# Two-layer graph attention: seven half products a pair in the projection, and another order at the turn of a tile in layer 1

## The chip, the cores and the metric

The kernel runs on one core of a Trainium2 chip. The metric is device time in microseconds (us), from one launch to its end, given as the median over runs. The engines work side by side, each through its own queue in the order of the program: TensorE (PE in the profile, its weight loads PEld), VectorE (DVE), ScalarE (ACT), GpSimd (POOL) and SyncE (SP). Transfers are issued from the queues of SP, ACT and POOL. A gather, with row numbers that are computed in the kernel, is issued from POOL.

## The reference

A graph of 10,000 nodes with 768 features, 160,000 edges and a self loop for each node goes through two layers of graph attention. The edges are sorted by target. In short:

```python
def gat_conv(x, edges, W, a_src, a_dst, bias, heads, out_ch, concat):
    xl = (x @ W).reshape(n, heads, out_ch)
    alpha_src = einsum('nhc,hc->nh', xl, a_src)
    alpha_dst = einsum('nhc,hc->nh', xl, a_dst)
    e = leaky_relu(alpha_src[src] + alpha_dst[dst], 0.2)
    e = exp(e - segment_max(e, dst)[dst])
    alpha = e / (segment_sum(e, dst)[dst] + 1e-16)
    out = segment_sum(xl[src] * alpha[:, :, None], dst)
    return (concat or mean over heads)(out) + bias

h  = relu(layer_norm(gat_conv(x, W1: 768 -> 4 heads x 256))) + x @ Wr1 + br1
h2 = layer_norm(gat_conv(h, W2: 1024 -> 768, one head)) + h @ Wr2 + br2
out = layer_norm(x + h2)
```

All numbers are float32.

## The kernel before

The nodes are cut into 79 tiles of 128. There are three stages: the projection, layer 1 and layer 2. The change touches the first two; layer 2 runs the same instructions before and after.

**Projection** (the loop over t at L669). For each tile, `product` multiplies the tile's x, which `load_x` has brought in already transposed as six blocks of 128x128, with W1 (six blocks of 128x1024). That makes twelve PE products of 128x128 by 128x512, into two PSUM banks. ACT copies the result to a row in SBUF (L674). DVE multiplies the result, from PSUM, with the two attention vectors (L677), ACT sums each head's 256 columns (L680), and POOL adds the bias (L682). SP stores the row to table1 (L684). Once per tile, `next(steps)` emits one step of two other pieces of work, which so share the engines with the projection: `prepare` builds the list of neighbours of every node, and `weight_steps` loads W2 and Wr1 and forms the attention columns of W2 (L659, L660). Steps of `prepare` that matter here: three counts a step, each of which compares 1408 sorted values per partition with a limit and sums the outcome (L240, DVE), whose results become the row numbers of a gather in the same step (L242, L245); one step with a comparison of 128x5056 and the start of running sums (L272, L277), continued in the next; steps of ranks (L324 to L331); scatters from POOL, six a step (L314); and twenty steps of neighbour lists, four gathers each (`listed`, L366 to L386, with the gathers at L393).

**Layer 1** (`ordered_layer1`). The nodes have been sorted by their number of neighbours, so that the 128 nodes of a tile have about as many: the number of slots of a tile goes from 8 up to 41 in the middle of the run and down to 9. Tiles of 14 to 19 slots are 43 of the 79. The rows of the neighbours (4 KB each) are gathered slot by slot into a ring of 29 (`Ring`, L425). A slot's place is free again once its row has been weighed. For one tile:

- `logits` (L478 to L490) needs all slots of the tile in the ring. It makes the exponents of the attention weights; POOL also takes the rank of each neighbour out of the rows (L489) and writes -BIG over the two attention entries and the rank (L490). `normalised` (L497 to L503) divides by the sum.
- The first `on_pe(t)` slots, one to four, are summed on PE with diagonal matrices of the weights (L739 on ACT, L745 on PE). Of the others, three of four are multiplied by their weights on ACT (L509) and added on DVE (L516), and one of four is done on DVE alone, head by head (L520).
- The last slot is added with an accumulated row sum (L826), from which ACT makes the mean and, with a pass of squares, the deviation (`deviation_about`, L590 to L594). DVE scales, shifts and adds the residual (L603, L605, L854).
- PE transposes h (L717), multiplies x with Wr1 for the residual (L172) and h with W2 in two parts: the first 512 columns in mid tile (`first_columns`, L775) and the last 258 columns at the next turn of a tile (`last_columns`, L790), between the transposes of x and those of the next h. ACT copies both parts out (L783, L796).

The order is written by hand (`manual_schedule`), and every engine follows it. The logits of tile t+1 begin five slots before the end of tile t where the ring has room (`EARLY`, `begin`), and then the first slot of tile t+1 that is not on PE is weighed ahead of the norm of tile t (`begun`). `ps_half` has two PSUM banks, which the transposes and both parts of the product with W2 share.

## Time and profile before

| What | Value |
|---|---|
| Median of 3 runs | 5480.69 us (5478.41 to 5491.34) |
| Profiled execution, its own time | 5480.69 us |
| Its span, first to last instruction | 5478.9 us |
| Mean granted clock of TensorE | 0.939 |
| Projection, products of x with W1 | 9 to 878 us |
| Layer 1 | about 895 to 3580 us |
| Layer 2 | about 3580 us to the end |
| Busy, share of the span | PE 87%, DVE 76%, POOL 60%, ACT 54% |

In the lines of the profile L172 is the line of the kernel, `out<-in` are the names of tiles, xN is a count, and the busy time and the mean duration of one instruction (in ns) follow. What stands behind a bar or in square brackets is the time for which the engine had nothing to do before the instruction, and what ended that time. A float32 product counts as two PE instructions in the profile. A busy share is a mean over stages: which engine a stage waits for has to be read inside the stage.

### The profile page before, as it was taken

The page shows a single profiled execution, that of the slowest core. Times are in us where ns is not written, and L with a number is a line of the kernel's source. Part 1 is how long each engine was busy: PE and PEld are TensorE (multiplying, and loading weights), DVE is VectorE, ACT ScalarE, POOL GpSimd, SP SyncE. Part 2 cuts the span into 40 slices and gives each one's busy share as a digit, 9 for nine tenths or more (in the row PEclk, how much of TensorE's full clock was granted, in tenths as well). Part 3 has the DMA queues.
Part 4 walks back from the last instruction along what each step waited for, and adds up shares of the span by engine and source line. Part 5 has one row for each costly group of instructions (what it writes and reads, how often), then busy time and mean ns, then how long its engine had stood idle before and what let it go on. Part 6 is the DMA issues. An engine that isn't in the chain of part 4 may idle for free. (4 is left out here: it accounts for less than half of the span.)

```text
span 5478.9 us, 58838 instructions
## 1 busy us (share of the span) xinstructions
PE 4753.3 (87%) x14847; PEld 2820.8 (51%) x14847; DVE 4186.5 (76%) x7350; ACT 2936.0 (54%) x8442; POOL 3267.3 (60%) x3407
## 2 busy tenths in 40 slices
PE   8999996998998876578898989999998865889998
PEld 3444443555555543344555545556666544566665
DVE  5784244788888777677788888759988766789998
ACT  3434344777788776677887777623333222233333
POOL 2446465555566655655666555257777666677774
PEclk9999998999999998889999999999999887899999
DMA  4333626899999988688999989589999988999995
GB/s 154 123 99 89 91 92 231 297 322 324 333 352 361 333 312 294 236 303 321 340 368 343 324 316 317 192 325 377 382 366 354 327 301 294 332 347 369 368 383 224
DMA packets 474304, 1591.33 MB, mean 290 GB/s; under 512 B 118327, under 2 KB 122487, under 8 KB 473958
## 3 DMA queue, kind: packets, MB, share of 16 engines
q0 software_dynamic: 322384, 1286.62, 65.7%
q1 hardware_dynamic: 149520, 297.43, 15.9%
q10 hardware_dynamic: 2054, 3.42, 0.2%
q8 instruction: 125, 2.05, 0.1%
q14 instruction: 221, 1.81, 0.1%
HBM read 1431.80 MB, written 177.29 MB: 294 GB/s over the span
## 5 line engine op out<-in xcount | busy, mean ns | idle before, releaser
L425 POOL DMA_INDIRECT ring<-table,slots x2675 | 2630.2, 983 | 1538.8 <-DVE acc L516 362.2
L520 DVE SCALAR_TENSOR_TENSOR acc<-ring,e,acc 128x512 f32<-128x512 f32 (+1 forms) x2506 | 1567.4, 625 | 161.6 <-PE acc L745 85.8
L509 ACT ACTIVATE ring<-ring,e 128x256 f32<-128x256 f32 x3480 | 1421.3, 502 | 0.0
L516 DVE TENSOR_TENSOR acc<-acc,ring 128x1024 f32<-128x1024 f32 x772 | 950.3, 1231 | 209.0 <-ACT ring L509 167.3
L991 PE MATMUL big<-ring,diagonals 128*128 128x256 f32 x2754 | 679.2, 409 | 202.5 <-ACT diagonals L990 183.8
L172 PE MATMUL big<-w,xT 128*128 128x512 f32 x1896 | 825.0, 597 | 26.7 <-DMA w<-in_W_dram 9.9
L172 PE MATMUL big<-wr,xT 128*128 128x512 f32 x1896 | 829.0, 594 | 0.2 <-ACT xT L718 0.2
L1005 PE MATMUL big<-wr,w 128*128 128x512 f32 (+1 forms) x2464 | 823.1, 487 | 0.0
L991 PEld LDWEIGHTS big<-ring,diagonals 128*128 128x128 f32 x2754 | 559.2, 206 | 319.9 <-ACT diagonals L990 223.0
L1005 PEld LDWEIGHTS big<-wr,w 128*128 128x128 f32 x2464 | 470.0, 191 | 329.5 <-issue 297.8
L172 PEld LDWEIGHTS big<-w,xT 128*128 128x128 f32 x1896 | 362.3, 192 | 485.3 <-issue 466.8
L745 PE MATMUL acc<-ring,diagonals 128*128 128x256 f32 x1568 | 399.9, 414 | 230.5 <-ACT diagonals L739 230.3
L172 PEld LDWEIGHTS big<-wr,xT 128*128 128x128 f32 x1896 | 355.3, 191 | 417.5 <-issue 416.8
L775 PE MATMUL half<-w,hT 128*128 128x512 f32 x1264 | 557.7, 594 | 0.0
L745 PEld LDWEIGHTS acc<-ring,diagonals 128*128 128x128 f32 x1568 | 322.7, 209 | 334.2 <-ACT diagonals L739 272.1
L990 ACT ACTIVATE diagonals<-ident,e 128x128 f32<-128x128 f32 x1377 | 410.9, 387 | 140.5 <-DVE e L500 124.7
L790 PE MATMUL half<-w,hT 128*128 128x258 f32 x1264 | 353.7, 441 | 150.4 <-ACT xT L718 150.4
L775 PEld LDWEIGHTS half<-w,hT 128*128 128x128 f32 x1264 | 239.8, 190 | 304.1 <-issue 287.3
L582 ACT ACTIVATE sd<-mv,eps 128x1 f32<-128x1 f32 x159 | 46.6, 293 | 637.3 <-DVE mv L580 637.2
L790 PEld LDWEIGHTS half<-w,hT 128*128 128x128 f32 x1264 | 273.3, 221 | 218.6 <-ACT xT L718 168.8
L677 DVE TENSOR_TENSOR scr<-big,ad_b 128x1024 f32<-128x1024 f32 x79 | 96.8, 1225 | 377.1 <-ACT row L674 377.1
L682 POOL TENSOR_TENSOR row<-row,none 128x1024 f32<-128x1024 f32 x79 | 187.0, 2367 | 265.9 <-ACT row L674 265.5
(184 smaller groups left out, 4062.0 us busy)
## 6 DMA issues: line engine op xcount, KB each, us to landing
ring<-table,slots POOLq DMA_INDIRECT x2675, 6.5
table<-row SPq DMA_DIRECT2D x79, 516.0 KB, 3.7
h_d<-hT SPq DMA_DIRECT2D x79, 512.0 KB, 6.6
w<-h_d SPq DMA_DIRECT2D x77, 512.0 KB, 8.4
table<-row SPq DMA_DIRECT2D x79, 385.0 KB, 6.0
ring<-table SPq DMA_DIRECT2D x79, 385.0 KB, 6.5
xT<-in_x_cols_dram SPq DMA_DIRECT2D x79, 384.0 KB, 4.6
x_d<-xt SPq DMA_DIRECT2D x79, 384.0 KB, 6.6
```

The costliest lines, as they stand in the source:

```text
L172: nc.tensor.matmul(p[:, c:e], aT[:, j, :], w[:, j, c:e], start=(j == 0), stop=(j == k - 1))
L425: nc.gpsimd.indirect_dma_start(out=to, out_offset=None, in_=table, in_offset=bass.IndirectOffsetOnAxis(ap=index, axis=0), **more)
L509: nc.scalar.activation(row[:, s], row[:, s], AF.Copy, scale=e[:, h:h + 1])
L516: nc.vector.tensor_add(acc[:, :c], acc[:, :c], row[:, :c])
L520: nc.vector.scalar_tensor_tensor(acc[:, s], row[:, s], e[:, h:h + 1], (acc if first is None else first)[:, s], op0=OP.mult, op1=OP.add)
L682: nc.gpsimd.tensor_add(row[:, :C1], row[:, :C1], b1_b)
L745: nc.tensor.matmul(acc[:, c:d], diagonals[:, k * H1 + i, :], ring.slot(q + k)[:, c:d], start=(k == 0 and c % BANK == 0), stop=(k == m - 1 ...
L775: nc.tensor.matmul(q, hT[:, j, :], w2[:, j, :BANK], start=(j == 0), stop=(j == K1 - 1))
L790: nc.tensor.matmul(q, hT[:, j, :], w2[:, j, BANK:R2], start=(j == 0), stop=(j == K1 - 1))
L990: nc.scalar.activation(diagonals[:, k % G, :], ident, AF.Copy, scale=e[:, k, :])
L991: nc.tensor.matmul(to, diagonals[:, k % G, :], ring.slot(FIRST[t] + k)[:, ON_PE2:C2], start=False, stop=(k == n - 1), skip_group_check=True)
L1005: nc.tensor.matmul(r[:, c:d], hT[:, j, :], wr2[:, j, c:d], start=False, stop=(j == K1 - 1 and d < C2), skip_group_check=True)
```

## The change

**Projection.** Tile 0 is multiplied as before. After it, tiles go in pairs. The pair's x (two tiles by two halves of the 768 rows) and W1 (two halves of rows by two halves of columns) are taken as 2x2 blocks, and their product is formed from seven block products instead of eight (Strassen's scheme), each of three PE products. DVE forms three sums and two in-place differences of blocks of W1 once, five sums of blocks of x for each pair, and seven combinations of the products into the two rows; ACT copies two of the products. DVE's multiplications with the attention vectors now read the row in SBUF. x is loaded four tiles ahead instead of two, and a pair's loads stand ahead of its stores in SP's queue. Both steps of a pair come at its end. Every second count runs on ACT, as a sum of signs and a small copy that halves it, and a count becomes a row number one step after it was made. Tiles of `prepare` share buffers.

**Layer 1.** The mean and the deviation come from DVE's statistics (`deviation`) again, there is no early first slot, the logits of the next tile begin three slots before the end, and the product with W2 is one piece in mid tile. `on_pe` gives one slot more to PE for tiles of 14 to 19 slots. The last slot is no longer always shared with ACT. What POOL did in `logits` is done by DVE.

```diff
+            def counts(j):
+                for i in range(j, min(j + STEP, NB)):
+                    less = pool2.tile([P, NA * P], BF16, name="less")
+                    if i % 2:
+                        nc.vector.tensor_scalar(less, most..., ids[:, i:i + 1], 0.0,
+                                                op0=OP.is_lt, op1=OP.add, accum_out=whole[:, i:i + 1])
+                        continue
+                    nc.scalar.activation(less, most..., AF.Sign, scale=-1.0,
+                                         bias=halves[:, i:i + 1], accum_out=whole[:, i:i + 1])
+                    nc.scalar.activation(whole[:, i:i + 1], whole[:, i:i + 1], AF.Copy, bias=0.5 * NA * P, scale=0.5)
...
-                nc.gpsimd.tensor_scalar(slots[:, a:b], rows[:, :, R1 - 1], -1.0, float(NP), op0=OP.mult, op1=OP.min)
-                nc.gpsimd.memset(rows[:, :, c + heads:], -BIG)
+                nc.vector.tensor_scalar(slots[:, a:b], rows[:, :, R1 - 1], -1.0, float(NP), op0=OP.mult, op1=OP.min)
+                nc.vector.memset(rows[:, :, c + heads:], -BIG)
...
-        for t in range(NT):
-            p = product(xTs.pop(t), w1, C1)
-            row = io.tile([P, R1], F32, name="row")
-            nc.scalar.copy(row[:, :C1], p[:, :C1])
...
+        def pair(t):
+            a1, a2 = (xTs.pop(i) for i in (t, t + 1))
+            a11, a12, a21, a22 = (a[:, k, :] for a in (a1, a2) for k in (upper, lower))
+            sums = io.tile([P, 5, KH, P], F32, name="sums")
+            for i, (a, op, b) in enumerate(((a11, OP.add, a12), (a21, OP.add, a22), (a11, OP.add, a22),
+                                            (a21, OP.subtract, a11), (a12, OP.subtract, a22))):
+                nc.vector.tensor_tensor(sums[:, i], a, b, op=op)
+            return a11, a22, sums
+        ready = pair(1)
+        for t in range(1, NT, 2):
+            a11, a22, sums = ready
+            r1, r2 = new_row(), new_row()
+            m3 = times(a11, b12)
+            m5 = times(sums[:, 0], b22)
+            nc.scalar.copy(r1[:, right], m5)
+            m2 = times(sums[:, 1], b11)
+            nc.scalar.copy(r2[:, left], m2)
+            nc.vector.tensor_sub(r2[:, right], m3, r2[:, left])
+            m4 = times(a22, b21)
+            nc.vector.tensor_sub(r1[:, left], m4, r1[:, right])
+            nc.vector.tensor_add(r1[:, right], r1[:, right], m3)
+            nc.vector.tensor_add(r2[:, left], r2[:, left], m4)
+            load_x(t + 4)
+            load_x(t + 5)
+            if t + 2 < NT:
+                ready = pair(t + 2)
+            m1 = times(sums[:, 2], bsums[:, 0])
+            nc.vector.tensor_add(r2[:, right], r2[:, right], m1)
+            m6 = times(sums[:, 3], bsums[:, 1])
+            nc.vector.tensor_add(r2[:, right], r2[:, right], m6)
+            times(sums[:, 4], bsums[:, 2], m1)
+            finish(t + 1, r2)
+            nc.vector.tensor_add(r1[:, left], r1[:, left], m1)
+            next(steps, None)
+            finish(t, r1)
             next(steps, None)
...
-                return min(max(SLOTS[t] // 2 - 6, 1), ON_PE1, SLOTS[t])
+                return min(max(SLOTS[t] // 2 - 5, 1), ON_PE1, SLOTS[t])
...
-                return (k - on_pe(t)) % SHARE > 0 or k == SLOTS[t] - 1
+                return (k - on_pe(t)) % SHARE > 0
...
                 if last:
-                    r_before, means, total = last
-                    h = pool.tile([P, C1], F32, name="h")
-                    if total is None:
-                        stats = deviation(small, pieces(means[:, :C1], BANK))
-                    else:
-                        stats, op = deviation_about(small, total, means[:, :C1], h), OP.add
-                begun = first + 1 if whole and early and n - 1 > first else first
-                for k in range(first, begun):
-                    multiplied(k + 1)
-                    weighed(k)
-                    ring.fetch(FIRST[t] + k + 1 + ring.size)
+                    r_before, means = last
+                    stats = deviation(small, pieces(means[:, :C1], BANK))
+                for _ in ahead:
+                    pass
+                if full is not None:
+                    store(t - 2)
                 moves = []
                 if live and t:
                     xT, moves = from_x(t)
-                q = last_columns() if full else None
+                multiplied(first + 2)
+                if last:
+                    h = pool.tile([P, C1], F32, name="h")
+                    scaled(h, [means[:, :C1]], stats, g1_b, be1_b)
+                    nc.vector.scalar_tensor_tensor(h, h, 0.0, r_before[:, :C1], op0=OP.max, op1=OP.add)
                 for move in moves:
                     move()
-                if last:
-                    scaled(h, [means[:, :C1]], stats, g1_b, be1_b, op)
-                    nc.vector.scalar_tensor_tensor(h, h, 0.0, r_before[:, :C1], op0=OP.max, op1=OP.add)
-                multiplied(first + 2)
-                if q is not None:
-                    store(q)
                 multiplied(first + LEAD)
...
                 def to_layer2():
+                    nonlocal full
                     nc.sync.dma_start(h1_d[t - 1], hT.rearrange("p k n -> p (k n)"))
-                    first_columns(t - 1, hT)
+                    full = []
+                    for c in range(0, R2, BANK):
+                        q = ps_half.tile([P, BANK], F32, name="half")[:, :min(BANK, R2 - c)]
+                        for j in range(K1):
+                            nc.tensor.matmul(q, hT[:, j, :], w2[:, j, c:c + q.shape[1]],
+                                             start=(j == 0), stop=(j == K1 - 1))
+                        full.append((c, q))
...
-                    if k >= begin:
-                        ready += list(itertools.islice(ahead, 1))[:2 - len(ready)]
-                    if k >= max(first, begun):
-                        weighed(k)
-                    if k >= begun or k < first:
-                        ring.fetch(FIRST[t] + k + 1 + ring.size)
+                    if n - LEAD <= k < n - LEAD + 2:
+                        ready += itertools.islice(ahead, 1)
+                    if k >= first:
+                        weigh(acc, ring.slot(FIRST[t] + k), e[:, k], DH1, shared=shared(t, k))
+                    ring.fetch(FIRST[t] + k + 1 + ring.size)
```

## The prediction

> **What bounds the kernel now.** I read the page first, then busy time by stage (windows whose edges I took from the first and last start of each line), then the timeline of single tiles. The profiled execution took 5480.69 us, of which its span is 5478.9; it is also the median of the runs (5478.41 to 5491.34), so the sum below goes against 5480.7. The page first: no engine is full over the span, so the stages have to be taken apart.
>
> ```profile
> PE 4753.3 (87%) x14847; PEld 2820.8 (51%) x14847; DVE 4186.5 (76%) x7350; ACT 2936.0 (54%) x8442; POOL 3267.3 (60%) x3407
> L677 DVE TENSOR_TENSOR scr<-big,ad_b 128x1024 f32<-128x1024 f32 x79 | 96.8, 1225 | 377.1 <-ACT row L674 377.1
> L682 POOL TENSOR_TENSOR row<-row,none 128x1024 f32<-128x1024 f32 x79 | 187.0, 2367 | 265.9 <-ACT row L674 265.5
> ```
>
> The windows (us; then busy us and count for PE, PEld, DVE, ACT, POOL; granted clock; DMA share; GB/s). The first four are the projection: PE is near full all along, but DVE's share goes from 22% to 79%. The last two are layer 1, tiles of 15 to 19 and of 20 to 26 neighbours: nothing is full, and DMA is at 0.94 and 0.87.
>
> ```profile
> 24.00:241.00 217.00, 206.10 (x476) 89.89 (x475) 154.66 (x198) 93.66 (x353) 89.39 (x62) 0.98 0.38 120
> 241.00:373.00 132.00, 131.18 (x314) 59.42 (x313) 103.61 (x137) 54.30 (x208) 66.18 (x50) 1.00 0.41 130
> 482.00:640.00 158.00, 158.00 (x369) 69.99 (x369) 35.46 (x31) 66.08 (x263) 87.75 (x70) 1.00 0.49 96
> 640.00:878.00 238.00, 230.94 (x535) 101.86 (x533) 108.02 (x437) 95.08 (x375) 127.16 (x101) 0.99 0.38 88
> 1180.00:1773.00 593.00, 534.28 (x1695) 311.97 (x1693) 505.56 (x770) 471.50 (x1230) 357.83 (x405) 0.96 0.94 340
> 1773.00:2186.00 413.00, 309.10 (x989) 186.77 (x990) 307.22 (x443) 300.23 (x789) 233.16 (x258) 0.90 0.87 316
> ```
>
> DVE's timeline in the first of them. L677 starts 11.45 us apart, not the 10.30 of POOL's L682 in the quiet stage (499.47, 509.77, 520.07): in 16 tiles the counts and the W2 column sums already pace the projection through DVE and ACT.
>
> ```profile
> 199.84 1.23 DVE L677 TENSOR_TENSOR scr<-big,ad_b 128x1024 f32<-128x1024 f32 x1 [1.90 <-ACT row L674]
> 202.11 1.67 DVE L240 TENSOR_SCALAR_CACHE_REDUCE less<-most,ids 128x1408 f32<-128x1408 f32 x1
> ...
> 208.44 0.95 DVE L659 TENSOR_TENSOR scr<-w,a 128x768 f32<-128x768 f32 x1
> 211.29 1.23 DVE L677 TENSOR_TENSOR scr<-big,ad_b 128x1024 f32<-128x1024 f32 x1 [1.90 <-ACT row L674]
> ```
>
> **Part 1, the projection.** PE loses 3 of 24 products a pair. One costs 10.30/12 = 0.858 us, so 2.57 us a pair, 100 us over 39 pairs if nothing else paces. DVE gains 7 operations of 128x512 (L327, the same size: 0.68, spaced 0.61) and 5 of 128x384 (L231: 0.56; plainer, I take 0.48): 6.7 us a pair. ACT's two copies halve (1.05 for 2.0). Half of the counts go to ACT: 80 of 1.72 on DVE become 40, and 40 on ACT that no row shows. From L660 (768 columns 0.84) and L680 (256, 0.40) 1408 columns give 1.4; with read and the halving copy 1.75; bounds 1.5 and 2.0.
>
> The order makes one ring of them, a pair long, because DVE's first subtraction needs ACT's copies of two products, which stand in ACT's queue behind the sums and counts of the last pair: DVE adds m7 (0.61), step one, two multiplications (2.28); ACT sums what the second of these made (1.6 past its half, 3.3 in all), its counts, two copies (1.05); DVE four operations on products (2.44), five sums (2.4), two adds (1.22), two multiplications (2.28). The tail from ACT's copies is 8.35. Before, a pair takes 20.6, and 22.9 where W2's sums run. By stage:
> - start: DVE must change two quarters of W1 after tile 0 read them (1.75 each by L677's rate) before the pair begins: +4, first pair -2;
> - 8 pairs with W2's sums: copies end 16.15 after the m7 add, so 24.5 for 22.9: +13;
> - 6.5 pairs of counts alone: 14.45 + 8.35 = 22.8 for 20.6, +14; the product of br1 with W2 (L172 on brT, 10.3 of PE) now finds PE idle and hides for the most part, -7;
> - 2 pairs with the running sums (64 of 0.19 and one of 5.43, all of them between DVE's parts of the ring): 29 and 27 for 22: +11; 3 pairs of ranks, two chunks of 2.3 us in each step: +5;
> - 5 pairs of scatters: POOL needs 2 x (2.37 + 6 x 1.27) = 20.0: -3; 4 quiet pairs, PE-bound at 18.0: -10;
> - 10 pairs with the lists of neighbours, steps of 2.6 on DVE: here the lock decides.
>
> The lock: L277 takes 0.19 each, but the second of these five started under POOL's add and ended with it:
>
> ```profile
> 383.38 3.13 DVE L277 TENSOR_TENSOR before<-before,hot 128x64 bf16<-128x64 bf16 x5
> 383.41 2.38 POOL L682 TENSOR_TENSOR row<-row,none 128x1024 f32<-128x1024 f32 x1 [7.93 <-ACT row L674]
> ```
>
> So an operation of DVE with two SBUF inputs waits for POOL's 2.37. Now POOL's add starts just ahead of each step, and the list steps are such operations: 2.5 + 2.6 + 2.28, again to 10.0, + 2.6 + 8.35 gives 20.7 for 20.6: +1. Without the lock these pairs run at PE's 18.0: -26. I take the first, as the row shows it.
> The Trainium skill ("SBUF — State Buffer", Who interferes with whom) has the same as a rule: a DVE instruction with two SBUF inputs and a GpSimd instruction that reads SBUF exclude each other for a whole instruction. It speaks against the change more widely than the row does, since the products' rows now lie in SBUF where L677 read PSUM: by the rule each second pair of multiplications also waits up to 1.9 us, in the quiet pairs at no cost (PE still ends last); where DVE paces it would add some 10 us, and the sum of the projection would be +36 for +26.
>
> Sum of the projection: +4 -2 +13 +7 +11 +5 -3 -10 +1 = **+26**, bounds -12 (no lock on the path, -31; counts at 1.5, 0.5 a pair in 14.5 pairs, -7) and +43 (counts at 2.0, +7; ten more from multiplications that wait). Earlier loads and stores hide: x lands in 4.6 us and is wanted a pair later.
>
> **Part 2, layer 1.** Its edits are one design against another. A tile of 17 neighbours:
>
> ```profile
> 1446.45 0.82 PE L717 MATMUL half<-ident,xt 128*128 128x128 f32 x6
> 1450.86 5.43 PE L790 MATMUL half<-w,hT 128*128 128x258 f32 x16 [3.59 <-ACT xT L718]
> 1456.33 0.37 ACT L796 COPY row<-half 128x258 f32<-128x258 f32 x1 [3.65 <-PE half L790]
> 1426.71 1.23 DVE L516 TENSOR_TENSOR acc<-acc,ring 128x1024 f32<-128x1024 f32 x1 [3.15 <-ACT ring L509]
> ```
>
> The last columns of W2's product stand at the turn of the tile: PE waits 3.59 for ACT's copies, ACT 3.65 for that product before it may weight the next rows, and DVE 3.15 for those (the last line is the same place one tile before). After, the whole product runs behind Wr1's, in mid tile, and this chain is gone. What is late next is DVE's own loop. Four neighbours take 2.13 + 3 x 1.33 (L520, L516, by their starts); logits 1.05, weights 1.15; added: slots and -BIG from POOL 0.45 (L489 0.29, L490 0.16), statistics 1.5 (L578, L580: 2 x 0.63 + 0.23) in place of 0.14 on the last add; then scale and residual 3.95. PE's loop: 0.8 + 10.3 + 10.6 + 0.85 + 1.75 a slot + 1.0 wait. One slot more on PE for 14 to 19 neighbours: PE +1.75, DVE -1.4, ACT -0.5. PE's loop is 27.0, 28.8 and 30.5 for two, three and four slots.
> - up to 13 neighbours (14 tiles), PE-bound at 26.0: 25.3 to 26.5, together -3; 14 neighbours (6): 27.0 for 27.2, 0;
> - 15, 16, 17 (23 tiles): 28.6, 28.8, 29.9; now the transposes of h stand 30.4, 30.4, 31.9 apart: -1.8 x 8 - 1.6 x 7 - 2.0 x 8 = -42;
> - 18 and 19 (14): 30.5 and 31.8 for 30.7 and 32.4, with DMA at 0.97 to 0.99: 0.
>
> From 20 on it is another chain, here of 22 neighbours:
>
> ```profile
> 1988.19 0.20 DVE L478 TENSOR_TENSOR e<-ring 128x36 f32<-128x36 f32 x1 [5.46 <-DMA ring<-table,slots]
> ...
> 1996.23 1.23 DVE L826 SCALAR_TENSOR_TENSOR acc<-ring,acc 128x1024 f32<-128x1024 f32 x1
> ...
> 2001.90 2.06 DVE L520 SCALAR_TENSOR_TENSOR acc<-ring,e,acc 128x256 f32<-128x256 f32 x4 [4.37 <-PE acc L745]
> 2003.87 1.28 DVE L603 SCALAR_TENSOR_TENSOR h<-acc,less,g 128x1024 f32<-128x1024 f32 x1
> ```
>
> DVE waits 5.46 for rows that could be asked for only when ring slots came free, and 4.37 for PE before the early first neighbour, with the norm (3.95) queued behind it. After, the norm fills that wait. The loop from PE's sums: 17.0 to free the slot, 8.5 to its landing, logits 1.5, one neighbour 1.33, weights 1.25, then PE's 16 products 10.8 (PE's row here is 9.76, later by the second half of the diagonals, which waits for the deviation): 40.4 for 42.0; 37.8 for 40.2 at 21; 33.2 for 35.3 at 20. The logits come two neighbours later, which the wait for DMA absorbs. 6, 4 and 4 tiles: -12, -10, -6; 23 and 24 (4): -8; the four largest 0.
>
> Sum -81. Loops added from rows leave waits out and the gathers move closer to a full DMA, so I take three quarters, **-60**; bounds -90 and +10.
>
> Together 5480.7 + 26 - 60 = **5446.7, say 5446**.
>
> **The rivals.**
> 1. *Layer 1 does not move* (slower): gathers land as late as DMA lets them. For: 0.94 DMA. Against: tiles of 18 run at 0.98 and 362 to 373 GB/s. Landing of 11 for 8.5 takes the gain of the large tiles, ACT 3 us late at the turn that of the middle ones: 5480.7 + 26 = 5507.
> 2. *PE paces the 43 tiles of 14 to 19* (slower still): each pays the slot, 43 x 1.75 = +75, and gains nothing; -31 stays for the rest: 5550. It decides once PE's wait for ACT's copies at the turn exceeds some 3 us; for it speaks the diagonals' second half, queued behind the deviation.
> 3. *The seven products pay*: DVE keeps up, no lock on the path, counts cheap: half to most of 100 arrives, -60 for +26: 5361. Against: DVE at 79% before 6.7 us a pair are added.
> 4. *The change does nothing in the projection* (0, not +26): 5421.
>
> **How the numbers follow.** Forecast 0.45, rival 1 0.20, rival 2 0.10, rival 3 0.10, rival 4 0.15. What a measurement can tell is 0.3%, 16 us: below 5464 is faster, above 5497 slower. Faster: 0.45 x 0.8 + 0.10 + 0.15 = 0.61; same: 0.45 x 0.15 + 0.04 of rival 1 = 0.11; the rest, 0.28, slower. The range leaves out most of rivals 2 and 3: 5385 to 5530; the forecast's own is 5410 to 5480.
>
> **What would show it.** Projection: L674's successor copies and DVE multiplications 24 to 25 us apart a pair while counts run, 18 in the quiet stage, 20 to 21 with the lists; its end near 905 for 878. Layer 1: no PE wait over 2 us for xT copies; tiles of 15 to 17 at 28.6 to 30 us; no DVE wait for PE's sums ahead of the norm. Wrong if DVE's wait for ACT's weighting stays, if the wait for gathered rows grows past 8 us, or if pairs run at 18 with counts in them.

## The result

The changed kernel takes 5409.5 us (median of four runs, 5396.95 to 5410.77) beside 5481.67 us for the kernel before (four runs): a ratio of 0.986, 95% interval 0.9841 to 0.9879. The gain is 72 us where the forecast had 35. Direction and range held, and by luck: the two terms of the sum did not hold, and their errors of +55 and -88 us cancel in part. The projection costs about three times what was forecast, and layer 1 gains well over twice as much. In some of the runs below layer 2, the same program throughout, takes 2182 to 2198 us instead of 1909 to 1915 and the kernel before 5777 to 5792 us instead of 5482 to 5487, so each run is read by its ratio to the kernel before in the same group, and by stage.

I cut both profiled executions (5480.69 and 5409.06 us) at the same two events, the first transposes of h on PE (tile 0 of layer 1 turns into tile 1) and the last ones.

| Stage | before, us | after, us | difference | forecast |
|---|---|---|---|---|
| to the first transposes of h ("projection" below) | 942.6 | 1023.9 | +81.4 | +26 |
| first to last transposes of h ("layer 1") | 2618.7 | 2470.8 | -147.9 | -60 (raw sum -81) |
| the rest (layer 2) | 1917.7 | 1912.5 | -5.2 | 0 |

On the page of after, DVE is the engine whose busy share rises most (84% for 76%), and its idle time before the adds of rows that ACT has weighted falls from 209.0 to 77.8 us (of which ACT's weighting ended 167.3 before and 8.8 now).

```profile
PE 4704.8 (87%) x14957; PEld 2814.3 (52%) x14957; DVE 4568.7 (84%) x8123; ACT 2826.2 (52%) x8306; POOL 3263.4 (60%) x3159
L528 DVE TENSOR_TENSOR acc<-acc,ring 128x1024 f32<-128x1024 f32 x801 | 985.7, 1231 | 77.8 <-ACT ring L521 8.8
```

The windows of after (us; then busy us and count for PE, PEld, DVE, ACT, POOL; granted clock; DMA share; GB/s). The first three are projection: four pairs with counts and W2's sums, four with counts alone, eight with lists of neighbours. The last two are layer 1, tiles of 15 to 19 and of 20 to 26 neighbours.

```profile
166.10:271.80 105.70, 82.64 (x168) 34.90 (x166) 87.55 (x120) 57.25 (x190) 47.85 (x33) 0.89 0.34 115
308.30:404.90 96.60, 79.67 (x169) 33.99 (x168) 81.13 (x114) 51.64 (x181) 45.16 (x33) 0.93 0.29 93
...
755.50:934.10 178.60, 154.76 (x337) 66.22 (x336) 147.28 (x417) 58.10 (x261) 106.85 (x80) 0.94 0.28 82
...
1254.00:1818.00 564.00, 539.12 (x1831) 323.41 (x1831) 518.73 (x848) 433.68 (x1166) 351.90 (x344) 1.00 0.97 356
1818.00:2200.00 382.00, 303.35 (x988) 183.89 (x986) 327.69 (x502) 283.01 (x753) 227.64 (x226) 0.90 0.93 344
```

In the projection PE, near full before, is idle for a fifth of the time while counts run, and DVE is at 83%: PE has three products fewer a pair, and nothing comes of it. In layer 1 the first window lasts 564 us for 590 before, PE at 96% and granted 1.00, and DMA moves 356 GB/s for 340.

Where the projection's time went is seen in one pair with W2's sums. The last of a pair's seven products is accumulated onto the first one, so PE can begin it only when DVE has read the first (L750), and DVE then adds it (L755). The timeline of after, DVE first, then ACT, then PE (start, us, engine, line, instruction; in brackets the idle time and what ended it):

```profile
140.52 0.69 DVE L755 TENSOR_TENSOR row<-row,m 128x512 f32<-128x512 f32 x1 [2.39 <-PE m L704]
...
150.30 1.73 DVE L253 CAST at<-whole 128x3 int32<-128x3 f32 x1
...
156.18 0.69 DVE L740 TENSOR_TENSOR row<-m,row 128x512 f32<-128x512 f32 x1 [2.24 <-ACT row L739]
...
166.10 0.69 DVE L755 TENSOR_TENSOR row<-row,m 128x512 f32<-128x512 f32 x1 [1.18 <-PE m L704]
...
155.10 0.56 ACT L737 COPY row<-m 128x512 f32<-128x512 f32 x1
155.56 0.58 ACT L739 COPY row<-m 128x512 f32<-128x512 f32 x1
...
150.85 5.31 PE L704 MATMUL m<-bsums,sums 128*128 128x512 f32 x12
161.79 4.27 PE L704 MATMUL m<-bsums,sums 128*128 128x512 f32 x6 [5.63 <-DVE row L750]
```

From one add of the seventh product (L755) to the next are 25.6 us. ACT's copies end 15.6 us after the first of them, where the forecast had 16.15. From there to the next add of the seventh product it had 8.35; the trace has 10.0. Of the difference of 1.6 us, 1.18 is DVE's wait for the seventh product: PE has stood idle for 5.63 us, waiting for DVE's add of the first product, and then three products take 4.27 us where six took 5.31. (At the rate of those six, an estimate, three would have been done 0.5 us before DVE was ready to add them.) The granted clock shows it, over the idle stretch and over the product after it:

```profile
156.20:161.70 5.50, 0.00 (x0) 0.00 (x0) 5.46 (x10) 0.00 (x0) 0.00 (x0) 0.96 0.51 169
161.79:166.10 4.31, 4.31 (x7) 2.02 (x8) 3.05 (x4) 2.28 (x11) 0.95 (x1) 0.66 0.00 0
```

Two more places cost much at once. The pair in which the product of br1 with W2 stands takes 36.5 us, since DVE adds two of its columns in the same step (timeline of after):

```profile
290.29 0.16 DVE L673 TENSOR_TENSOR lift<-row 128x1 f32<-128x1 f32 x1 [12.59 <-ACT row L672]
```

And DVE waits for the gathered windows of the neighbour lists, which one step asks for and the next wants (groups of instructions from 140 us to the end of the projection; busy and mean ns, then the idle time before them and what ended it):

```profile
L385 DVE TENSOR_TENSOR less<-window,named 128x80 f32<-128x80 int32 (+13 forms) x20 | 11.2, 561 | 34.1 <-DMA window<-in_src_dram,begin 34.1
```

In layer 1 the view of waits, tiles of 15 to 19, shows what went. Before (us in total, times, longest):

```profile
PE half L790 <- ACT xT L718: 48.4, 19, 4.5
DVE acc L516 <- ACT ring L509: 51.8, 36, 4.5
ACT row L796 <- PE half L790: 59.7, 20, 5.0
```

and after, where no wait of DVE for ACT's weighting is left among them:

```profile
PE half L790 <- ACT xT L791: 10.1, 17, 1.0
PE acc L818 <- ACT diagonals L812: 8.2, 14, 0.8
...
DVE acc L532 <- PE acc L818: 4.8, 9, 0.6
```

### The profile page after: what moved, and what is told of

Same layout as the page of the kernel before. It is cut to its first block, busy times and chain, and to the rows that moved or that the text cites. A ratio compares the mean times of both kernels' runs of the same rounds, so it can differ in the third digit from the quotient of the medians.

```text
span 5407.2 us, 59694 instructions
## 1 busy us (share of the span) xinstructions
PE 4704.8 (87%) x14957; PEld 2814.3 (52%) x14957; DVE 4568.7 (84%) x8123; ACT 2826.2 (52%) x8306; POOL 3263.4 (60%) x3159
## 5 line engine op out<-in xcount | busy, mean ns | idle before, releaser
L521 ACT ACTIVATE ring<-ring,e 128x256 f32<-128x256 f32 x3284 | 1337.8, 508 | 0.0
L528 DVE TENSOR_TENSOR acc<-acc,ring 128x1024 f32<-128x1024 f32 x801 | 985.7, 1231 | 77.8 <-ACT ring L521 8.8
L911 PE MATMUL half<-w,hT 128*128 128x512 f32 (+1 forms) x2528 | 830.4, 486 | 0.0
L818 PE MATMUL acc<-ring,diagonals 128*128 128x256 f32 x1912 | 477.9, 407 | 194.7 <-ACT diagonals L812 194.4
L818 PEld LDWEIGHTS acc<-ring,diagonals 128*128 128x128 f32 x1912 | 385.5, 205 | 279.9 <-ACT diagonals L812 219.8
L692 ACT ACTIVATE scr<-scr 128x256 f32<-128x256 f32 x632 | 253.5, 403 | 488.9 <-DVE scr L689 488.9
L1022 ACT ACTIVATE diagonals<-ident,e 128x128 f32<-128x128 f32 x1377 | 411.0, 387 | 141.5 <-DVE e L512 128.9
L704 PE MATMUL m<-bsums,sums 128*128 128x512 f32 x702 | 360.6, 665 | 128.5 <-DVE row L750 128.5
L812 ACT ACTIVATE diagonals<-ident,e 128x128 f32<-128x128 f32 x956 | 293.0, 387 | 202.4 <-DVE e L512 202.4
L498 ACT ACTIVATE e<-e 128x68 f32<-128x68 f32 (+29 forms) x160 | 38.2, 239 | 631.5 <-DVE e L497 602.8
L704 PEld LDWEIGHTS m<-bsums,sums 128*128 128x128 f32 x702 | 144.1, 211 | 329.6 <-issue 165.3
```

Source lines behind the costliest of these rows:

```text
L521: nc.scalar.activation(row[:, s], row[:, s], AF.Copy, scale=e[:, h:h + 1])
L528: nc.vector.tensor_add(acc[:, :c], acc[:, :c], row[:, :c])
L704: nc.tensor.matmul(to, a[:, k, :], b[:, k, :], start=(p is None and k == 0), stop=(k == a.shape[1] - 1), skip_group_check=True)
L812: nc.scalar.activation(diagonals[:, k * H1 + i, :], ident, AF.Copy, scale=e[:, k, i:i + 1])
L818: nc.tensor.matmul(acc[:, c:d], diagonals[:, k * H1 + i, :], ring.slot(q + k)[:, c:d], start=(k == 0 and c % BANK == 0), stop=(k == m - 1 ...
L911: nc.tensor.matmul(q, hT[:, j, :], w2[:, j, c:c + q.shape[1]], start=(j == 0), stop=(j == K1 - 1))
```

## The experiments

Fifteen kernels ran, in five groups (runs 1 to 4, 5 to 8, 9 to 12, 13, and 14 with 15), each group beside the kernel before. The projection of after takes 1023.9 to 1029.1 us in the executions that leave it alone, and its layer 1 2467 to 2475.

**1 and 2. Each half alone.** The first kernel keeps the projection of before and takes layer 1 of after; the second does the reverse.

> The projection of before with layer 1 of after. Theory A, read off the two traces: the stages add up, the projection pays 81 us and layer 1 gains 148, the rest 5; then this kernel takes 5481 - 148 - 5 = 5328 us (5315 to 5345). Theory B: the sizes of the forecast (+26 and -60) were right and the stages help each other, layer 1 running better because of what the new projection leaves behind (clock, transfers); then it takes 5400 to 5420.

> The projection of after with layer 1 of before. Theory A: 5481 + 81 = 5562 us (5550 to 5575), slower than before by 1.5%. Theory B, the forecast's +26: 5507 us (5495 to 5515).

Measured: layer 1 alone 0.9714 of before (0.9687 to 0.9741), projection 946.3 and layer 1 2472.3 us; projection alone 1.0143 (1.0117 to 1.0169), projection 1029.1 and layer 1 2636.7. On the time of before the ratios give 5325 and 5560 us, near the 5328 and 5562 of theory A. The stages add up: by the medians of their group (5616.79 and 5864.98 beside 5777.02 us) the differences are -160 and +88 us, together -72, what the change does; by the ratios they are -157 and +78, together -79. The projection of after is a loss, and the sizes of the forecast fall, not its additivity.

**3. Lists two steps behind their gathers.**

```diff
-                for r in asked:
-                    listed(*r)
-                asked = [(t, window)]
+                while len(asked) > 1:
+                    listed(*asked.pop(0))
+                asked.append((t, window))
                 yield
-            yield
```

> After, with each list of neighbours made two steps behind its gathers instead of one. Theory A: DVE waits 34 us in all for the windows (10.9 in the first of the ten pairs, 1.1 to 3.7 in the others), because the two steps of a pair stand 3 us apart; that goes, the pairs come down to 20 to 21 us, and the kernel gains 20 to 34: 5375 to 5389 us. Rival: the lock between DVE's list operations and POOL's add paces these pairs, as the forecast had it; then only the first pair gains, and the time is 5400 to 5409.

Measured: 0.9819 of before (0.9794 to 0.9844), projection 1010.9 us, a gain of 13 and so between the two, nearer to the rival: the first pair with lists comes from 32.9 to 19.0 us, and the next eight only from 22.3 to 21.8 on the mean. No wait for a window is left, but DVE's busy time in those pairs rises from 18.4 to 20.6 us. Beyond the first pair the wait was only taking the place of something else.

**4. ACT's sums behind the next pair's copies.** The sums and the store of the pair's last row are put off until ACT has copied two products of the next pair, and one of the two steps stands ahead of the other row's multiplications. (`finish` is split for this: it keeps the multiplications and POOL's add, and `sums_and_store` has the rest.)

```diff
             nc.scalar.copy(r2[:, left], m2)
+            sums_and_store(*late)
...
-            finish(t + 1, r2)
+            next(steps, None)
+            sums_and_store(*finish(t + 1, r2))
             nc.vector.tensor_add(r1[:, left], r1[:, left], m1)
             next(steps, None)
-            finish(t, r1)
-            next(steps, None)
+            late = finish(t, r1)
```

> After, with ACT's sums of a pair's last row (and its store) put behind the two copies of the next pair, and one of the two steps put ahead of the multiplications of the other row. Theory A, the ring: DVE waits for ACT's copies behind those sums and counts (2.2 to 5.2 us a pair in most pairs); the waits go, pairs with W2's sums come from 26.5 to about 24, pairs with counts alone from 24.1 to 22, scatters from 21.3 to 20; in all -20 to -45, 5365 to 5389 us. Rival: what paces the pairs is DVE's own work with POOL's add in its way (22 us busy, some 2 us more that no wait explains); then the waits only move to another place and the time stays within 8 us of 5409.

Measured: 0.9693 of before (0.9667 to 0.9718), projection 937.3 us. The gain of 87 us there is twice what I expected of the ring. A pair with W2's sums in its timeline, DVE then PE:

```profile
134.71 0.68 DVE L761 TENSOR_TENSOR row<-row,m 128x512 f32<-128x512 f32 x1
...
142.37 0.68 DVE L745 TENSOR_TENSOR row<-m,row 128x512 f32<-128x512 f32 x1
...
156.20 0.68 DVE L761 TENSOR_TENSOR row<-row,m 128x512 f32<-128x512 f32 x1
...
147.96 5.49 PE L708 MATMUL m<-bsums,sums 128*128 128x512 f32 x6 [3.20 <-DVE row L755]
```

Neither the subtraction that wants ACT's copies (L745) nor the add of the seventh product (L761) waits any more: 21.5 us a pair for 26.4, of which DVE is busy 21.1. PE still idles and still runs its next products slowly, but the moved step lies over that. DVE's own work is the bound.

**11. The moved step alone.** Only the first half of that edit: the step moves, ACT's order stays.

> After, with only the first of a pair's two steps moved, from behind the add of the seventh product to ahead of the multiplications of the pair's other row; ACT's order of sums and copies stays. Theory A: the seventh product comes late because PE, after an idle of 5 us, runs it at a lower clock (4.3 us for 2.6); the moved step covers that wait (1.2 to 2.4 us a pair) and no more, since the ring through ACT's copies is as long as before: projection 1024 - 30 = 994 us (985 to 1005). Rival: what the fourth run gained (87 us) came from the moved step and not from ACT's order: projection below 960 us.

Measured: 0.9845 of before (0.9829 to 0.9862), projection 1018.1 us, a gain of 6 where I expected 30. The wait for the seventh product is gone, but the order now puts the first multiplication of one row beside POOL's add for the other, and it takes 3.59 us for 1.22 (DVE and POOL, the same stretch of the timeline):

```profile
149.57 3.59 DVE L689 TENSOR_TENSOR scr<-row,ad_b 128x1024 f32<-128x1024 f32 x1
...
149.71 2.36 POOL L694 TENSOR_TENSOR row<-row,none 128x1024 f32<-128x1024 f32 x1
```

POOL's add starts 0.14 us behind the multiplication, by the profile's start times, and the multiplication ends 1.09 us behind the add. The run changes two things, one of them not meant, and so says little of the ring. Runs 14, 10 and 15 separate them.

**14. ACT's sums put off, the steps left alone**, from the twelfth pair on: the first and last lines of run 4's edit.

> After, with ACT's sums of a pair's last row (and its store) behind the two copies of the next pair, from the twelfth pair on, where W2's sums are done; the steps stay where they are. Theory A, the ring through ACT's queue paces: in the pairs with counts alone the wait for the copies (2.2 us) goes, 24.1 comes down to 22 us, the 1.4 us of the late seventh product stay; scatters and lists gain up to 1 us a pair; projection 1024 - 15 to 35 us. Rival, the late seventh product and POOL's add pace: these pairs stay at 23.5 us and more, projection 1015 or more.

Measured: 0.9803 of before (0.9778 to 0.9828), projection 1004.7 us, 19 less and so inside theory A's range. The pairs with counts alone come from 24.1 to 20.9 us, more than the 2.2 of the wait: the wait for the seventh product, which theory A let stay, went too. ACT's order alone takes the ring away there; DVE, busy for 20.1, is the bound, with no wait from one add of the seventh product (L762) to the next in its timeline. PE, of which the last line is, now idles 2.15 us instead of 5.63 ahead of that product, and its three PE products take 2.84 us instead of 4.27:

```profile
352.41 0.68 DVE L762 TENSOR_TENSOR row<-row,m 128x512 f32<-128x512 f32 x1
...
364.13 0.68 DVE L747 TENSOR_TENSOR row<-m,row 128x512 f32<-128x512 f32 x1
...
372.84 0.68 DVE L762 TENSOR_TENSOR row<-row,m 128x512 f32<-128x512 f32 x1
...
369.72 2.84 PE L708 MATMUL m<-bsums,sums 128*128 128x512 f32 x6 [2.15 <-DVE row L757]
```

**10. No add of the bias.** POOL's add is left out, and with it the addition of b1 to the projected rows.

```diff
-            nc.gpsimd.tensor_add(row[:, :C1], row[:, :C1], b1_b)
```

> After, without POOL's add of the bias b1 to the projected rows (a part of the computation is left out). Theory A, the lock of the forecast: operations of DVE that stand still beside this add (a cast of 3 columns takes 1.7 us beside it and 0.17 elsewhere) are on the ring; without it the pairs with counts lose 1.5 us each and the pairs with lists up to 2.6: projection 1024 - 26 - 20 = 978 us (965 to 1000). Rival, the ring runs through ACT's queue and PE, and what DVE loses beside the add it would spend waiting for ACT's copies: projection 1012 to 1026 us.

Measured: 0.9757 of before (0.974 to 0.9773), projection 963.7 us. Its windows, for the same kinds of pairs as above (with W2's sums, counts alone, scatters, lists):

```profile
165.30:271.00 105.70, 82.62 (x168) 34.91 (x166) 81.67 (x121) 57.24 (x191) 27.81 (x24) 0.89 0.34 115
307.50:404.00 96.50, 79.58 (x169) 33.95 (x168) 74.75 (x113) 51.53 (x181) 24.77 (x24) 0.93 0.28 93
556.40:647.30 90.90, 90.90 (x212) 39.42 (x211) 58.50 (x81) 37.68 (x171) 36.92 (x33) 1.00 0.39 103
734.00:879.80 145.80, 145.80 (x338) 63.20 (x338) 134.14 (x416) 58.07 (x261) 76.05 (x63) 1.00 0.34 100
```

Each theory holds in a stage of its own, and neither total does (965 to 1000 and 1012 to 1026 were expected). In the pairs with counts, where theory A had a gain of 1.5 us each, DVE is busy 6 us less over each stretch, and the stretch is as long as in after to 0.1 us: DVE spends on waits what it saves beside the add. In the pairs with lists and scatters PE is full, 18.2 us a pair, and 18.0 is what the forecast named for a pair without the lock. Not all of the 4.1 us that go from a pair with lists are the lock. DVE's busy time falls by 1.6 us a pair (147.28 and 134.14 over eight pairs); its waits for windows, 19.4 us over the eight pairs in after, are gone as well, and in after POOL's add stands in the same queue that asks for the windows.

**15. The moved step, without POOL's add**: the edits of runs 11 and 10 together, so that b1 is again not added.

> After, with the step moved ahead of the multiplications of the other row (as in the eleventh run) and without POOL's add of the bias (left out of the computation, as in the tenth). Measured against the tenth run, where pairs with W2's sums take 26.3 us, pairs with counts alone 24.1, and the projection ends at 964. Theory A, the late seventh product is a term of the ring: the moved step covers it, pairs come to 24.3 and 22.7 us, projection 964 - 25 = 940. Rival, the ring through ACT is as long without that wait, DVE only waits longer for the copies: 26 and 24 us stay, projection 955 or more.

Measured: 0.9744 of before (0.9722 to 0.9766), projection 938.8 us. Theory A, to 0.2 us: 24.5 and 22.8 us a pair, the two numbers of the forecast's ring, with the wait for the copies still in it (timeline of DVE).

```profile
166.91 0.68 DVE L755 TENSOR_TENSOR row<-row,m 128x512 f32<-128x512 f32 x1
...
177.57 0.69 DVE L739 TENSOR_TENSOR row<-m,row 128x512 f32<-128x512 f32 x1 [3.53 <-ACT row L738]
...
191.42 0.68 DVE L755 TENSOR_TENSOR row<-row,m 128x512 f32<-128x512 f32 x1
```

So the ring without that wait is as long as forecast, and what the forecast lacked was the late seventh product.

The pairs side by side, in us from one add of the seventh product to the next (means over the pairs of a kind, without the first of those with W2's sums, 24.0 in after, and the last with lists; the moved step brings each kind about one pair earlier):

| Pairs | forecast | after | run 3 | run 4 | run 14 | run 11 | run 10 | run 15 |
|---|---|---|---|---|---|---|---|---|
| counts and W2's sums | 24.5 | 26.4 | 26.3 | 21.8 | 26.6 | 26.8 | 26.3 | 24.5 |
| br1's product | 22.8 and a rest | 36.5 | 36.9 | 34.1 | 37.5 | 37.9 | 36.5 | 35.7 |
| counts alone | 22.8 | 24.1 | 24.2 | 20.4 | 20.9 | 25.2 | 24.1 | 22.8 |
| scatters | 20.0 | 21.3 | 21.3 | 20.4 | 20.6 | 20.5 | 18.2 | 18.4 |
| quiet | 18.0 | 18.3 | 18.3 | 18.4 | 17.8 | 18.5 | 18.2 | 18.2 |
| first with lists | 20.7 | 32.9 | 19.0 | 24.5 | 29.3 | 25.7 | 32.1 | 25.6 |
| other lists | 20.7 | 22.3 | 21.8 | 20.3 | 22.3 | 21.1 | 18.2 | 18.5 |

**5. The product with W2 in two pieces at the turn again**, on after's layer 1.

```diff
                 moves = []
                 if live and t:
                     xT, moves = from_x(t)
-                multiplied(first + 2)
+                q = last_columns() if full else None
+                for move in moves:
+                    move()
                 if last:
...
-                for move in moves:
-                    move()
+                multiplied(first + 2)
+                if q is not None:
+                    store(q)
```

> After, with the product with W2 cut in two again: 512 columns in mid tile, 258 at the turn of a tile between the transposes of x and those of h, and the order of the turn that goes with it (copies of x's transposes ahead of the norm and of the first weighted rows). Layer 1 took 2471 us in after and 2619 in before. Theory A, the forecast's reason: this chain at the turn (PE waits for ACT's copies, ACT for that product, DVE for ACT) was what the old order paid for, so layer 1 goes back by 60 to 110 us, tiles of 15 to 17 neighbours to 30 us and more, and PE waits over 2 us for the copies of xT again. Rival, the gain came from the slot moved to PE, or from what moved between POOL, ACT and DVE: less than 30 us are lost here, and more than 60 in one of the next three.

Measured: 1.0177 of before (1.016 to 1.0194); layer 1 takes 2648.9 us, 178 more than after, where 60 to 110 were expected, and 30 more than before. Of the chain that the forecast named, two links are there again, in the waits of the tiles of 15 to 19 neighbours: ACT waits for the last columns, and DVE for ACT's weighting. The third is not: PE waits at most 1.0 us for the copies of xT, where theory A had over 2.

```profile
ACT row L861 <- PE half L855: 37.4, 19, 2.0
ACT xT L791 <- PE half L790: 36.4, 16, 4.3
...
DVE acc L528 <- ACT ring L521: 51.2, 40, 2.7
...
PE half L855 <- ACT xT L791: 10.4, 19, 1.0
```

Tiles of up to 15 neighbours lose next to nothing (0.2 us on the mean), those of 16 and 17 lose 2.2 to 2.6 us each, those of 18 to 20 3.5 to 5, and larger ones 2.6 to 3.7. That is in good part not where the forecast had put the gain: it had 0 for 18 and 19.

**6. One slot fewer on PE**, as before: `SLOTS[t] // 2 - 6` for `- 5`.

> After, with the number of slots summed on PE back to that of before (one fewer for tiles of 14 to 19 neighbours and for those of 20 to 22 as far as the cap allows). Theory A, DVE's own loop paces the tiles of 15 to 19 in after: each pays 1.0 to 1.4 us, layer 1 loses 35 to 60 us. Rival, PE paces them in after: each gains up to 1.75 us, layer 1 gains 20 to 75.

Measured: 0.9955 of before (0.9938 to 0.9972); layer 1 2525.5 us, a loss of 55. Theory A holds for 14 to 19 neighbours (1.2 to 1.4 us a tile from 15 to 17, 0.8 to 0.9 at 18 and 19, 2.0 at 14). From 20 to 22 nothing moves; there the cap of four slots on PE (`ON_PE1`) gives the same number either way. PE now waits for h, which comes from DVE (waits in the tiles of 15 to 19):

```profile
PE half L790 <- DVE h L889: 27.0, 12, 2.4
PE acc L818 <- ACT diagonals L812: 19.1, 14, 2.6
```

**7 and 8. Two moves to DVE undone**: the two small operations of logits on POOL again, and the mean from the last add with ACT's pass of squares again.

> After, with the two small operations of logits (ranks out of the gathered rows, -BIG over their ends) back on POOL. Theory A, DVE's loop paces: DVE is rid of 0.45 us a tile, layer 1 gains 10 to 25 us. Rival, POOL's queue matters: the same queue issues the gathers, the operations wait there for ACT's exponents and hold up the gathers behind them; then layer 1 loses 10 to 60 us, and DVE's or PE's waits for gathered rows grow.

> After, with the mean taken from the sums of the last add on DVE and the deviation from a pass of squares on ACT, and the last slot always shared with ACT, as before. Theory A, DVE's loop paces: DVE is rid of 1.4 us a tile, and ACT, with room, takes 1.3 more: layer 1 gains 20 to 60 us. Rival, what matters is when the deviation is there: ACT's pass stands ahead of the weighting of the next rows and the norm waits for it; layer 1 stays within 10 us or loses up to 60.

Measured: 0.9816 (0.98 to 0.9833) with layer 1 at 2450.8 us, and 0.9837 (0.9821 to 0.9853) with 2459.1 us. Theory A holds for the first, 20 us; the second gives 12, less than its range, and gains it at 15 to 17 neighbours while those of 20 lose 0.7 us a tile. Both moves were small losses inside the change: 1.8% and 1.6% faster than before stand beside the change's 1.4%. The 12 us are not much beside the 8 by which layer 1 of after varies between runs.

**12. The early logits and the early first slot again.**

```diff
+                begun = first + 1 if whole and early and n - 1 > first else first
+                for k in range(first, begun):
+                    multiplied(k + 1)
+                    weigh(acc, ring.slot(FIRST[t] + k), e[:, k], DH1, shared=shared(t, k))
+                    ring.fetch(FIRST[t] + k + 1 + ring.size)
...
-                    if n - LEAD <= k < n - LEAD + 2:
+                    if k >= begin:
```

> After, with the logits of the next tile begun five slots before the end of a tile again, and its first slot that is not on PE weighed ahead of the norm, where the ring has room. Theory A, the forecast's chain for 20 neighbours and more: DVE waits there for PE's sums with the norm queued behind, so each of those 18 tiles loses 1.5 to 3 us, and tiles of 15 to 19 lose 0 to 1: layer 1 2471 + 30 to 60 us. Rival, that wait was only due to the product at the turn: layer 1 stays within 10 us of 2471 or gains.

Measured: 1.0584 of before (1.0566 to 1.0602); layer 1 2862.7 us, a loss of 392 where I expected 30 to 60, and not in the tiles that I had named: those of 11 to 19 neighbours lose 5.4 to 7.4 us each, those of 20 lose 3.6, 21 to 23 1.2 to 2.8, and those of 24 and more nothing. DVE waits for PE's sums of the next tile with the norm behind it, and PE then waits for h (waits in the tiles of 15 to 19):

```profile
PE half L791 <- DVE h L896: 97.6, 18, 5.4
...
DVE acc L533 <- PE acc L819: 133.1, 19, 8.5
```

So the parts of layer 1, undone one at a time, give +178, +392, +55, -20 and -12, which is far from 148.

**13. Both of the turn's parts back together**, the edits of runs 5 and 12.

> After, with both put back: the product with W2 cut in two with its order of the turn (as in the fifth run) and the early logits and first slot (as in the twelfth). Theory A, the two belong together: PE, which in the twelfth run waited 5.4 us a tile for h, has the 5.4 us of the last columns to do there, and what is left is the old order's own chain. Counted back from before by the other parts (2619 - 55 + 20 + 12), layer 1 takes 2596 us (2570 to 2620), less than with either alone. Rival, each costs by itself: layer 1 takes 2863 us or more.

Measured: 1.0062 of before (1.0042 to 1.0081), layer 1 2580.7 us: less than with either alone, and in the range of theory A. PE's wait for h is small again, for the last columns stand in it, and so is DVE's for PE's sums (the same tiles):

```profile
PE half L791 <- DVE h L909: 15.4, 13, 1.2
...
DVE acc L533 <- PE acc L819: 15.8, 15, 1.8
DVE acc L529 <- ACT ring L522: 4.0, 11, 0.6
```

The old order was one design; the change replaced both parts at once, and that was worth 110 us (2580.7 to 2470.8). With 55 for the slot, less 20 and 12 for the two moves, 133 of the 148 us are accounted for; 15 are not. By number of neighbours, in us a tile (from one group of transposes of h to the next):

| Neighbours | tiles | before | after | run 5: W2 split | run 12: early slot | run 13: both | run 6: slot back |
|---|---|---|---|---|---|---|---|
| 9 to 13 | 13 | 26.30 | 24.91 | 25.10 | 30.89 | 26.18 | 24.89 |
| 14 | 6 | 27.40 | 26.16 | 26.46 | 33.60 | 27.49 | 28.16 |
| 15 to 17 | 23 | 30.94 | 28.79 | 30.44 | 34.64 | 28.99 | 30.05 |
| 18 and 19 | 14 | 31.55 | 30.82 | 35.09 | 37.41 | 31.53 | 31.68 |
| 20 to 22 | 14 | 38.62 | 36.03 | 39.50 | 38.65 | 39.25 | 35.92 |
| 23 to 26 | 6 | 45.46 | 42.79 | 46.23 | 43.76 | 46.09 | 43.32 |

**9. What helped, together**: the edits of runs 3, 4 and 7 (not that of run 8), and br1's sum taken by DVE a step later, from two columns that ACT copies for it.

> After, with four edits: the sums behind the copies and the step moved (as in the fourth run), the lists two steps behind their gathers (as in the third), br1's attention sum taken by DVE a step later than ACT copies its product, and the two small operations of logits on POOL (as in the seventh). Theory A, the stages and the edits add up: projection 937 - 6 (the one window wait that is left) - 9 (DVE's wait of 12.6 us for br1's product, less what PE itself needs) = 922 us; layer 1 2451; layer 2 as before: 5288 us (5275 to 5305), a ratio of 0.965. Rival, DVE is the bound of the projection by now and the waits only change places: 937 stays, 5303 us or more.

Measured: 5295.08 us (5292.27 to 5297.55), 0.965 of before (0.9634 to 0.9666), so 2.1% less than the change. Layer 1 2448.1, layer 2 1912.3 us. The projection, 935.3 us instead of 922, is all that fails: the wait for br1's product only changes its place, to the buffer from which that product reads, and the windows' wait had little left to give. The timeline of DVE in that pair:

```profile
252.81 1.23 DVE L691 TENSOR_TENSOR scr<-row,as_b 128x1024 f32<-128x1024 f32 x1 [11.07 <-PE m L670]
```

With these edits the new projection is worth 942.6 - 935.3, 7 us, where PE saves 100, and 7 us is little beside the 4 by which the projection of before differs between its two profiles (942.6, and 946.3 in run 1). DVE paces most pairs.

## Why the prediction was right and wrong

**The projection, +26 for +81.** The mechanism was right: a ring through DVE and ACT while counts run (run 14 opens it), POOL's add in the way of the lists (run 10), PE pacing only the quiet pairs (18.3 measured, 18.0 forecast). The step that failed is the sizing of four terms; the differences are sums over the pairs of each kind.

- "The tail from ACT's copies is 8.35" holds no wait for the seventh product. It measures 10.0 in the pair shown; over eight pairs with W2's sums 209 us for 196, over those with counts alone 5 more. Run 15, with that wait covered and no lock, has the forecast's 24.5 and 22.8. I took PE's products at their full clock in a stage where my own ring, 24.5 us for 18.0 of products, left PE idle for 6 us a pair.
- "Now finds PE idle and hides for the most part, -7": the product does not hide, as DVE takes its result in the same step. One pair of 36.5 for 22.8 and a rest of about 3, 10 to 14 us. I looked for PE's idle time and not for who reads the product.
- "+1" for the lists took the lock alone. The first of those pairs adds 12 us for gathers that the next step wants at once (without that wait, in run 3, the pair takes 19.0 us instead of 32.9), the other nine 1.6 each. The two steps of a pair stand closer together than the steps of two tiles did; the forecast moved the steps and did not follow the gathers that they issue.
- The running sums, ranks and scatters came out at 59.6, 74.5 and 106.7 us for 56, 67 and 100: 18 together.

That makes some 74. Against it stand the first pair and the one behind the counts, 40 us for the 52 that the forecast's stages leave over. So the pairs explain about 62 where the sum was 55 short (911 us from the first add of a seventh product to the last, for some 850), and the rest, in the start and the end, I have not taken apart. The forecast's sign for the end was the last product of x with W1 near 905 us; it ends at 956.

Two sums of the forecast are off by a little: 29 and 27 for 22 twice are +12, not +11, and the lower bound takes 31 for the lock where its own lines give 27.

The forecast also weighed a rule of the Trainium skill ("SBUF — State Buffer", Who interferes with whom): by it, each second pair of multiplications should wait for POOL's add. In after they have a median of 1225 and 1218 ns, so most don't (six of the 138 after 140 us take 3.0 to 4.0 us): in the pair shown, they run while POOL has no add under way (they end at 148.79, and its add starts at 149.63). Run 11, where the two start within 0.14 us of each other, shows the rule: 3.59 us. The rule was right and the order of the two engines in this kernel kept it out. What does stand still in after is an operation that I had not priced, the cast of three counts to row numbers: 1.73 us beside POOL's add as the median of 14, 0.17 in the other 13. The same section of that page names copies and casts among the operations that can take the shared ports; for this cast the trace agrees. In the pairs with counts it costs nothing, by run 10.

**Layer 1, -60 for -148.** Taking "three quarters" of the sum was the first wrong step, and cost 21 us: the forecast's reason was that loops made from rows leave out waits, but the waits of the old order went too. The second is in the raw sum: -81 is little over half of what was measured, since it has nothing for tiles of 14, 18 and 19 neighbours and for the four largest, and too little for those of 9 to 13 and from 20 on. By the tiles:

| Neighbours | forecast, raw | measured | what the runs show |
|---|---|---|---|
| 9 to 13 | -3 | -18 | the turn (run 13: -1.5 with the old one) |
| 14 | 0 | -7 | slot and turn |
| 15 to 17 | -42 | -49 | the slot on PE; the turn adds 5 (run 13: -45) |
| 18 and 19 | 0 | -10 | the turn (run 13: 0) |
| 20 to 22 | -28 | -36 | the turn (run 13: +9) |
| 23 to 26 | -8 | -16 | the turn (run 13: +4) |
| 27 and 41 | 0 | -11 | over half the turn (run 13: -5) |

(Measured is from before to after, in us over all tiles of the row.)

The signs that the forecast named for layer 1 came: in the tiles of 15 to 19 neighbours no wait of PE for the copies of xT is over 1.0 us, and those of 15 to 17 take 28.2 to 29.7 us, for 28.6 to 30. They don't tell the causes apart.

For 15 to 17 neighbours the number was near and the reason wrong. "This chain is gone" was to give the 42; but with the old order of the turn back and all else of the change kept (run 13), these tiles still gain 45, and without the extra slot on PE (run 6) 29 us of the gain go. In run 13 two waits of that chain are small although its order is there: PE waits 3.6 us for the copies of xT and DVE 4.0 for ACT's weighting, where before had 48.4 and 51.8; ACT still waits 36.6 us for the last columns. Beside the slot it keeps the two moves to DVE, the deviation's pass off ACT among them; what of the shrunken waits is due to each was not separated. For 20 neighbours and more the sizes were short by a quarter to a half, and the reason is only in part shown. DVE's wait for PE's sums does fall, as forecast, and its wait for rows too (35.5 to 19.8 us, tiles of 20 to 26). But the early first slot does not bring the first one back: in run 12 it is 11.9 us, and what returns is the wait for rows. The same tiles in before, after and run 12 (the last two lines):

```profile
DVE acc L520 <- PE acc L745: 21.6, 6, 4.5
...
DVE acc L532 <- PE acc L818: 8.9, 9, 1.7
...
DVE e L491 <- DMA ring<-table,slots: 35.6, 10, 5.6
DVE acc L533 <- PE acc L819: 11.9, 8, 2.7
```

And W2's split alone costs these tiles more than the early slot alone: 3.5 us a tile for 2.6 from 20 to 22 neighbours, 3.4 for 1.0 from 23 to 26, where both together cost 3.2 and 3.3. The forecast's chain is thus one of two, and not the larger. That the early slot alone costs 392 us, 349 of them in tiles of up to 19 neighbours, the forecast could not see, since in the old order the product at the turn lay in PE's wait.

"0" at 18 and 19 neighbours, for a DMA share of 0.97 to 0.99, was wrong by 10 us: over the tiles of 15 to 19 DMA still went from 340 to 356 GB/s. The operations from POOL and the statistics were rightly counted as costs of DVE; they are 20 and 12 us (runs 7 and 8).

**The rivals.** 1 (layer 1 does not move) and 4 (the projection costs nothing) fall with runs 1 and 2. 2 (PE paces the tiles of 14 to 19 with its added slot, +75) is refuted by run 6, by which the slot gains 55. 3 (the seven products pay) falls for this order of ACT's queue, and with the order of run 9 the projection as a whole gets 7 us.

## What to carry to other kernels

Work taken off the engine that is full comes to nothing where it is paid in operations of an engine that closes a ring with another one: write down the ring, queue by queue, with the wait at each hand-over, before counting the saving; here the new projection lost 81 us in one order of ACT's queue and its steps and came out even, within 5 to 7 us, in another. A step that is moved takes its gathers along, so look for who wants what it asks for, and when. And parts of a tuned order should not be judged one at a time: two that cost 178 and 392 us alone cost 110 together, because the one filled the wait that the other made.

## What the hardware showed unexpectedly

PE's granted clock falls to a half when PE has been idle for a few us, and this shows in the durations: after idles of 4.2 to 6 us in the pairs with counts, the first 4 us of products were granted 0.50 to 0.64, and three products took 4.27 us in the pair shown, instead of half of the 5.31 that six took. The Trainium skill ("TensorE: Matmul & The Clock Gate", The HAM clock gate) gives a gate of that kind, half rate after an idle window of about 3.4 us. For these idles the runs agree, and so does run 14, where an idle of 2.15 us left the product at 2.84 us; but in layer 1 of before, half-rate stretches follow idles of 1.9 to 2.7 us as well (0.50 from 1328.35 to 1331.7 us, after an idle of 2.65). The runs show besides where such a kernel pays for it: not in PE's time, of which there is enough, but in what the first product after the idle holds up. From 140 us on DVE waited 33.8 us for seventh products. In layer 1 the effect goes the other way. With PE's waits of 2.5 us a tile (48.4 over 19) gone, the tiles of 15 to 19 neighbours run at 1.00 where they had 0.96: the trace of before has twelve stretches at 0.50 there, each after an idle of PE, and that of after one.

Layer 2 goes with the chip. The record names the chip of each group: runs 1 to 4 ran on chip 5 and runs 13 to 15 on chip 6, and there layer 2 has a granted clock of 0.88; runs 5 to 8 ran on chip 12 and runs 9 to 12 on chip 9, with 0.93. Over the whole of layer 2, run 1 moved 297 GB/s and after 340, for the same bytes. The projection and layer 1 differ by less than 1% between the chips (2470.2 us in run 3, 2467.3 in run 10). Why the chips differ stays open.
